# Layer 2's edge lookups in a two-layer graph attention kernel: another order of loads around them

## The chip, the cores and the metric

The kernel runs on one core of a Trainium2 chip. The metric is device time in microseconds. Three runs of the kernel before gave 1846.12, 1849.89 and 1850.75 us; their median, 1849.89 us, is the time before.

A core has five engines that run side by side: TensorE (PE in the profile) multiplies matrices, VectorE (DVE) does elementwise work and reductions, ScalarE (ACT) activations and copies, GpSimd (POOL) here mostly issues indirect DMAs (gathers), and SyncE (SP) issues plain DMAs. Each engine has its own instruction queue and keeps the order of that queue. The DMA transfers that SP, ACT and POOL issue share 16 DMA engines.

## The reference, cut to what matters

The input is a graph of 3125 nodes with 768 features each, and 53125 edges (25000 random ones, both ways, and a loop at each node), sorted by destination. A layer norm and a ReLU come first; then two graph attention layers (GAT). In short:

```
def gat_conv(x, edge_index, W, a_src, a_dst, bias, heads, out_ch, concat):
    src, dst = edge_index with a loop added at every node
    xl = (x @ W).reshape(n, heads, out_ch)
    alpha_src, alpha_dst = (xl * a_src).sum(-1), (xl * a_dst).sum(-1)
    e = leaky_relu(alpha_src[src] + alpha_dst[dst], 0.2)
    m = segment_max(e, dst)
    e = exp(e - m[dst])
    s = segment_sum(e, dst)
    alpha = e / (s[dst] + 1e-16)
    return segment_sum(xl[src] * alpha[:, :, None], dst) + bias

h0 = relu(layernorm(x))
h1 = relu(layer_norm(gat_conv(h0, ..., W1, heads=4, out_ch=256), g1, be1)) + (h0 @ Wr1 + br1)
h2 = layer_norm(gat_conv(h1, ..., W2, heads=1, out_ch=768), g2, be2) + (h1 @ Wr2 + br2)
out = x + h2
```

All matrices are float32. Layer 1 has 4 heads of 256 columns, layer 2 one head of 768. The edges' own order is kept in tiles: the nodes are split into 25 tiles of 128 destinations (the last one has 53), and a tile's edges fill up to 17 slots of 128 edges.

## The kernel before

Only layer 2 and the end of layer 1 are of interest. Layer 1 ends with its last tile's product with W2: the row of `xl` goes to the DRAM table `table2`, and the two numbers per node, alpha_src and alpha_dst, go to the SBUF tile `asad2` (L1261). Then layer 2 runs in three stages.

**Lookups** (`for b in range(NB)`, L1341 and on). For every edge slot of the 25 tiles, alpha_src of the source and alpha_dst of the destination are looked up with one-hot matrices, which layer 1 left in DRAM (`hot_d`, float8). For tile b, `load_hot` (L1283) brings one matrix `hot` of 405.1 KB into one of four buffers. `source_values` (L542) multiplies it with the table `tabs` on PE (51 small matmuls, L551), masks the result into `pick` on DVE (L553) and reduces it into `wide` (L556); `own_products` and `own_values` (L528, L539) do the same for the destinations (5 matmuls, then a reduction into the tile `own`). The first four matrices are loaded by POOL at the end of layer 1, behind eight pieces of the weights `wr2` (L1280, L1285); the other 21 by SP, each as soon as an earlier lookup has released its buffer.

**Shares** (`shares`, L643). The looked-up values become softmax weights: five transposes on PE (L673), two scans over the edges on DVE for the maximum per destination (L680, L681), six transposes back (L686), and some elementwise work, an exponential on ACT among it. `pen`, a mask, is loaded from DRAM by SP (L660).

**Sums** (`sums`, L703, called at L1376). For every tile and each of its slots POOL gathers 128 rows of `table2` (L774, tile `g`, 26 buffers, 416 gathers in this layer), DVE builds a weight matrix (L796), and PE adds the weighted rows into PSUM (L821). At a tile's end DVE adds the node's own row, which SP has loaded (`load_rows`, L191), normalizes, and ACT stores the tile of the output (`end2`, L1366).

**Residual.** `h1 @ Wr2` plus its biases is added to x. `load(b)` (L1291) loads a tile's h1 (512 KB) and x (384 KB) through SP, `residual` (L1300) does the matmuls in eight steps (L1307), a bias matmul (L1311) and two DVE adds into `xr` (L1316). It's a generator: each `next` does one step. `ahead_of(first, end, apart)` strings tiles together and loads two tiles ahead. Two tiles (`FIRST = 2`) are done ahead of the sums: a step after each lookup from b = 5 on, the rest in `shares`, whose last argument says how many steps stand behind the first transposes and how many behind the transposes back. The other 23 are spread evenly over the sums (`each`, L1359).

**What sets the order.** PE keeps the order in which the program is written; in the sums ACT and DVE do too. The other engines' queues are ordered by a planner, which runs a model of the machine at compile time and, whenever an engine is free, gives it the earliest written instruction that waits for nothing. A DMA that is written late but needs only a free buffer can so be issued early. `with tc.issue_after(ins):` puts the instructions written inside it behind `ins` where they are on the same engine. It's used once: the gathers (POOL) come after `behind`, a small copy on POOL that reads `wide` after the 18th lookup (b = 17, L1352).

Of the kernel before, what the change touches and what calls it, by code (L numbers as in the profile page):

```python
# [9 lines left out]
F32 = mybir.dt.float32  # L10
F32R = mybir.dt.float32r
BF16 = mybir.dt.bfloat16
# [17 lines left out]
J = 17  # L30
S = J * 128
# [4 lines left out]
WIN = 640  # L36
# [32 lines left out]
def in_order(  # L69
# [16 lines left out]
    nc = tc.nc  # L86
# [4 lines left out]
    C2 = W2.shape[1]  # L91
    P = 128
    NB = -(-N // P)
# [3 lines left out]
    NK1, NK2 = D // 128, HC // 128  # L97
# [18 lines left out]
    def rows_of(b):  # L116
        return P if b < NB - 1 else LAST

    def cols_of(i):
        return sum(rows_of(b) for b in late_in[i])  # L120
# [10 lines left out]
    h1T_d = dram.tile([NB, 128, NK2, P], F32, name="h1T_d")  # L131
# [9 lines left out]
    hot_d = dram.tile([NB, 128, HOT], F8, name="hot_d")  # L141
# [38 lines left out]
    def bcast(vec, n, parts=P):  # L180
        return bass.AP(tensor=vec.tensor, offset=vec.offset, ap=[[0, parts], [1, n]])
# [35 lines left out]
    def bias_rows(pool, name):  # L217
        t = pool.tile([2, C2], F32R, name=name)
        nc.sync.dma_start(t.bitcast(F32), parts_d)
        return t  # L220
# [616 lines left out]
    with tc.tile_pool(name="m1", bufs=1) as mp:  # L837
# [8 lines left out]
        with tc.tile_pool(name="h0", bufs=1) as hp, tc.tile_pool(name="pm1", bufs=1, space=PSUM) as pm1, \  # L846
# [5 lines left out]
            so = right.enter_context(tc.tile_pool(name="so1", bufs=1, side="right"))  # L852
            own = so.tile([128, J, 2 * H, NB], F32, name="own")
            tabs = so.tile([P, 3, H, NB], BF16, name="tabs")
            cnt = so.tile([128, NB], F32, name="cnt")
            with tc.tile_pool(name="w1", bufs=1) as wp, tc.tile_pool(name="d1", bufs=2) as dp, \
# [216 lines left out]
                fill = early()  # L1073
# [11 lines left out]
            with tc.tile_pool(name="pq1", bufs=1, space=PSUM) as pp:  # L1085
                with tc.tile_pool(name="sb1", bufs=1) as sb:
                    n = J * H * NB
                    pick = scr[:, :n].rearrange("p (j h b) -> p j h b", h=H, b=NB)
# [71 lines left out]
        with tc.tile_pool(name="w2", bufs=1, reuse_waits="tile") as wp, tc.tile_pool(name="e1", bufs=2, reuse_waits="tile") as ep, \  # L1160
# [3 lines left out]
            def load(i, k, q=nc.sync):  # L1164
                if i < NG:
                    n = cols_of(i)
                    t = loaded[i, k] = wp.tile([128, WIDE], F32, name="h0k", bufs=11)
                    q.dma_start(t[:, :n], h0T_d[i][:, k, :n])
# [98 lines left out]
    with tc.tile_pool(name="m2", bufs=1, reuse_waits="tile") as mp, \  # L1267
            tc.tile_pool(name="pr2", bufs=1, space=PSUM, reuse_waits="tile") as pr:
        al2 = mp.tile([128, J, 1, NB], F32, name="al2")
        ends2 = mp.tile([128, J, NB, 3], F32, name="ends2")  # L1270
        nc.vector.memset(ends2[:, :, :, 0:1], 1.0)
        ball_r = bias_rows(mp, "ball_r")
        b2_b = mp.tile([P, C2], F32, name="b2_b")
        g2_b = mp.tile([P, C2], F32, name="g2_b")
        wide = mp.tile([128, J, NB], F32, name="wide")
        FIRST = 2
        xrs = {0: mp.tile([128, C2], F32, name="xr", bufs=FIRST + 4)}
        wr2 = mp.tile([128, NK2, C2], F32, name="wr2")
        for k in range(NK2):
            nc.gpsimd.dma_start(wr2[:, k, :], Wr2[k * 128:(k + 1) * 128, :])  # L1280
        hots = {}

        def load_hot(b, q):  # L1283
            hots[b] = mp.tile([128, HOT], F8, name="hot", bufs=4)
            q.dma_start(hots[b][:, :S + WIN + J * NB], hot_d[b, :, :S + WIN + J * NB])  # L1285

        for b in range(4):
            load_hot(b, nc.gpsimd)
        loaded = {}

        def load(b):  # L1291
            if b < NB and b not in loaded:
                h1 = mp.tile([128, NK2, P], F32, name="h1", bufs=3)
                r = rows_of(b)
                nc.sync.dma_start(h1[:, :, :r], h1T_d[b][:, :, :r])
                xr = xrs[b] = xrs.get(b) or mp.tile([128, C2], F32, name="xr", bufs=FIRST + 4)
                load_rows(nc.sync, xr, x, b)
                loaded[b] = h1, xr

        def residual(b, apart):  # L1300

            h1, xr = loaded.pop(b)
            r = rows_of(b)
            pms = [pr.tile([P, 512], F32, name=f"pr{i}", bufs=2)[:r] for i in range(2)]
            for k in range(NK2):
                for i, pm in enumerate(pms):
                    nc.tensor.matmul(pm[:, :384], h1[:, k, :r], wr2[:, k, i * 384:(i + 1) * 384],  # L1307
                                     start=(k == 0), stop=False)
                yield
            for i, pm in enumerate(pms):  # L1310
                nc.tensor.matmul(pm[:, :384], ones_r[:, :r], ball_r[:, i * 384:(i + 1) * 384], start=False, stop=True)  # L1311
            for _ in range(apart):
                yield
            for i, pm in enumerate(pms):
                cs = slice(i * 384, (i + 1) * 384)
                nc.vector.tensor_add(xr[:r, cs], pm[:, :384], xr[:r, cs])  # L1316

        def ahead_of(first, end, apart):
            load(first)
            load(first + 1)  # L1320
            for b in range(first, end):
                load(b + 2)
                yield from residual(b, apart)

        with tc.tile_pool(name="ps2", bufs=1, space=PSUM, reuse_waits="tile") as pp:
            fill = ahead_of(0, FIRST, 5)
            with tc.tile_pool(name="so2", bufs=1, side="right", reuse_waits="tile") as so, \
                    tc.manual_schedule(engines={PE}):
                own = so.tile([128, J, 2, NB], F32, name="own")
                al = wide[:, :, None, :]  # L1330
                with tc.tile_pool(name="sb2", bufs=2, side="right", reuse_waits="tile") as sb:
                    part = parts_of(sb, asad2.rearrange("p b v -> p (b v)"), NB * 2, "part")
                    tabs = sb.tile([P, 3, 1, NB], BF16, name="tabs", bufs=1)
                    tabd = sb.tile([P, NB, 4, 3, 2], BF16, name="tabd", bufs=1)
                    v = lambda i: part[:, i, :].rearrange("p (b v) -> p b v", v=2)
                    by_quarter(tabd, v, NB, 1)
                    for i in range(3):
                        nc.vector.tensor_copy(tabs[:, i], v(i)[:, :, :1].rearrange("p b h -> p h b"))
                    for b in range(NB):
                        if b not in hots:  # L1340
                            load_hot(b, nc.sync)  # L1341
                        hot = hots.pop(b)
                        pick = sb.tile([128, J, 1, NB], F32, name="pick")
                        source_values(1, al, b, pp, 3, J, hot, tabs,
                                      hot[:, S + WIN:S + WIN + J * NB].rearrange("p (j b) -> p j b", b=NB), pick)
                        own_values(own, b, own_products(1, pp, hot[:, S:S + WIN], tabd[:, b]))
                        if b in (1, 2):
                            load(b - 1)
                        if b > 4:
                            next(fill)  # L1350
                        if b == NB - 8:
                            behind = nc.gpsimd.tensor_copy(mark, al[:, 0, 0, b:b + 1]).ins  # L1352
                with tc.tile_pool(name="sr2", bufs=1, side="right", reuse_waits="tile") as sr:
                    shares(wide, own, al2[:, :, 0, :], ends2, sr, pp, fill, (3, 2))
                for _ in fill:
                    pass

        more = ahead_of(FIRST, NB, 3)
        each = (NB - FIRST) * (NK2 + 3) / ((NB - 1.5) * len(ROUNDS))  # L1359

        with tc.tile_pool(name="w3", bufs=1, reuse_waits="tile") as wp, tc.tile_pool(name="e2", bufs=2, reuse_waits="tile") as ep, \
                tc.tile_pool(name="g2", bufs=1, reuse_waits="tile") as gp, tc.tile_pool(name="pg2", bufs=1, space=PSUM, reuse_waits="tile") as pp:
            nc.sync.dma_start(b2_b, bcast(b2, C2))
            nc.sync.dma_start(g2_b, bcast(g2, C2))

            def end2(b, z, share):  # L1366
                nc.vector.scalar_tensor_tensor(z, z, share, b2_b[:z.shape[0]], op0=OP.mult, op1=OP.add)  # L1367
                yield from norm_steps(ep, z, C2, 1)
                mu, rstd = norm_steps.found
                nc.vector.scalar_tensor_tensor(z, z, mu, g2_b[:z.shape[0]], op0=OP.subtract, op1=OP.mult)  # L1370
                nc.vector.scalar_tensor_tensor(z, z, rstd, xrs[b][:z.shape[0]], op0=OP.mult, op1=OP.add)
                yield
                store_rows(nc.scalar, out, b, z)

            with tc.issue_after(behind):
                sums(1, C2, table2, al2, ends2, 26, 1, gp, pp, end2, more, [each] * len(ROUNDS))  # L1376


# [470 lines left out]
```

## Time and profile before

| what | value |
|---|---|
| median of three runs | 1849.89 us |
| the profiled execution's own time | 1853.64 us |
| its span, first to last instruction | 1851.8 us |
| mean granted TensorE clock | 0.976 |
| PE busy | 1741.8 us (94% of the span) |
| DVE busy | 1063.1 us (57%) |
| POOL busy | 908.4 us (49%) |
| ACT busy | 296.2 us (16%) |
| DMA, mean over the span | 310 GB/s |
| first lookup, first gather, first sum of layer 2 | 1236.60, 1289.97, 1321.43 us |

Times in the profile are microseconds from the first instruction; "L1307" is a line of the kernel. An instruction group reads as line, engine, operation, output<-inputs, count; what stands in brackets or behind "<-" is what ended the idle time before it. "SPq" is SyncE's queue. The chain of waits follows the work that ended last back from the end. A row of a table by stage has the busy time (and number) of PE, PE's weight loads, DVE, ACT and POOL, then the granted clock (1.00 is full speed), the busy share of the DMA engines and what they moved. Matmuls are pipelined, so a busy PE isn't PE at its peak.

### The profile page before, as it was taken

To read this page: it belongs to the slowest core of one execution; us is meant where nothing else is said; L and a number is where in the kernel's file an instruction comes from. 1 tells how busy PE (TensorE), PEld (TensorE's weight loads), DVE (VectorE), ACT (ScalarE), POOL (GpSimd) and SP (SyncE) were. 2 spreads that over 40 slices of the span, in tenths; PEclk is the share of its full clock that TensorE was granted. 3 is DMA by queue.
4 is the path that set the end of the run, shared out by engine and by line. 5 is a ranking of instruction groups with operands and counts; after the bars stand their busy time and mean duration, and the time that the engine had idled before them with its cause. 6 is when DMAs were issued, how large, how long until landed. Compare 5 with 4: busy or idle time off the path is not lost. (4 is left out here: it accounts for less than half of the span.)

```text
span 1851.8 us, 34112 instructions
## 1 busy us (share of the span) xinstructions
PE 1741.8 (94%) x12558; PEld 965.8 (52%) x12558; DVE 1063.1 (57%) x3030; ACT 296.2 (16%) x1094; POOL 908.4 (49%) x981
## 2 busy tenths in 40 slices
PE   8999999999878999999999999979899999999996
PEld 5666665566434656556555555547444333334331
DVE  7683434888825465566566646534565444555555
ACT  2222331000211212112212112110111000001100
POOL 2000111111166666666666666501777777777774
PEclk9999999999989999999999999988899999999998
DMA  7824537776199999999999999937999999999996
GB/s 236 286 82 153 145 97 202 177 189 146 61 399 407 406 393 400 385 406 380 409 410 393 410 410 357 382 133 241 332 383 373 384 370 378 381 381 385 372 351 231
DMA packets 180209, 574.86 MB, mean 310 GB/s; under 512 B 32767, under 2 KB 54265, under 8 KB 179908
## 3 DMA queue, kind: packets, MB, share of 16 engines
q0 software_dynamic: 108432, 408.37, 59.5%
q1 hardware_dynamic: 68074, 154.62, 24.0%
q10 hardware_dynamic: 3530, 9.60, 1.3%
q8 instruction: 103, 1.69, 0.4%
q14 instruction: 70, 0.57, 0.1%
HBM read 503.27 MB, written 73.85 MB: 312 GB/s over the span
## 5 line engine op out<-in xcount | busy, mean ns | idle before, releaser
L774 POOL DMA_INDIRECT g<-table,idx_s x832 | 819.3, 985 | 416.4 <-issue 150.0
L821 PE MATMUL pa<-g,w 128*32 128x256 f32 (+2 forms) x5868 | 501.5, 426 | 50.8 <-DMA g<-table,idx_s 35.9
L821 PEld LDWEIGHTS pa<-g,w 128*32 128x32 f32 x5868 | 191.4, 110 | 328.7 <-issue 145.7
L1307 PE MATMUL pr<-wr,h 128*128 128x384 f32 (+1 forms) x800 | 290.7, 504 | 0.0
L1254 PE MATMUL p<-w,h1T 128*128 128x384 f32 (+2 forms) x800 | 280.4, 499 | 2.6 <-DVE h1T L1240 2.6
L796 DVE TENSOR_SCALAR w<-iota_f,rel_s,al 128x32 f32<-128x32 f32 (+1 forms) x416 | 104.1, 325 | 232.4 <-PE pa L821 231.9
L1307 PEld LDWEIGHTS pr<-wr,h 128*128 128x128 f32 (+1 forms) x800 | 141.8, 189 | 140.2 <-issue 59.7
L1254 PEld LDWEIGHTS p<-w,h1T 128*128 128x128 f32 (+1 forms) x800 | 144.9, 188 | 123.3 <-issue 26.4
L801 DVE TENSOR_TENSOR w<-oh,al 128x128 f32<-128x128 f32 (+1 forms) x416 | 132.0, 317 | 92.8 <-PE pa L821 59.9
L1185 PE MATMUL pr<-h0k,wr 128*128 128x256 f32 (+1 forms) x576 | 141.1, 393 | 0.0
L926 PE MATMUL pm<-w,h0l 128*128 128x344 f32 (+1 forms) x468 | 140.8, 455 | 0.0
L1063 PE MATMUL pm<-h0g,wr 128*128 128x512 f32 x288 | 133.1, 610 | 0.0
L926 PE MATMUL pm<-w,h0g 128*128 128x344 f32 x432 | 130.6, 458 | 0.3 <-ACT h0g L905 0.3
L1185 PEld LDWEIGHTS pr<-h0k,wr 128*128 128x128 f32 x576 | 106.9, 191 | 29.6 <-issue 9.8
L994 POOL DMA_DIRECT2D hot_d<-ohd x25 | 13.5, 540 | 220.1 <-DVE own L502 124.0
L800 DVE TENSOR_SCALAR oh<-iota_f,rel_s 128x32 f32<-128x32 f32 (+1 forms) x416 | 112.1, 269 | 0.1
L926 PEld LDWEIGHTS pm<-w,h0l 128*128 128x128 f32 (+1 forms) x468 | 84.8, 185 | 44.1 <-issue 5.7
L491 ACT ACTIVATE bn_sd<-bn_mv,eps 128x1 f32<-128x1 f32 (+1 forms) x50 | 14.7, 294 | 554.6 <-DVE bn_mv L487 537.8
L926 PEld LDWEIGHTS pm<-w,h0g 128*128 128x128 f32 x432 | 81.7, 193 | 40.6 <-issue 1.4
L1063 PEld LDWEIGHTS pm<-h0g,wr 128*128 128x128 f32 x288 | 53.6, 194 | 57.5 <-issue 57.2
L1238 ACT ACTIVATE h1T<-p,be_c,g_c 128x128 f32<-128x128 f32 (+1 forms) x200 | 72.2, 475 | 15.6 <-PE p L1233 12.5
L553 DVE TENSOR_TENSOR scr<-pq,ohh 128x500 f32<-128x500 f32 x100 | 56.8, 596 | 20.3 <-PE pq L551 20.3
(306 smaller groups left out, 1415.4 us busy)
## 6 DMA issues: line engine op xcount, KB each, us to landing
s<-slo_d SPq DMA_DIRECT2D x25, 544.0 KB
g<-table,idx_s POOLq DMA_INDIRECT x832
table<-row SPq DMA_DIRECT2D x24, 512.0 KB
own<-table SPq DMA_DIRECT2D x24, 512.0 KB
h1T_d<-h1T SPq DMA_DIRECT2D x24, 512.0 KB
h<-h1T_d SPq DMA_DIRECT2D x24, 512.0 KB
ring<-in_x_dram SPq DMA_DIRECT2D x24, 384.0 KB
table<-row SPq DMA_DIRECT2D x24, 384.0 KB
```

What stands on the lines that cost most here:

```text
L553: nc.vector.tensor_tensor(pick[:, j0:j0 + n], q, ohh[:, j0:j0 + n, None, :].to_broadcast([128, n, heads, NB]), OP.mult)
L774: nc.gpsimd.indirect_dma_start(out=g[:, :width], out_offset=None, in_=table[:, :], in_offset=bass.IndirectOffsetOnAxis(ap=idx_s[:, b * J + ...
L796: nc.vector.tensor_scalar(w[:, 0, :], iota_f[:, lo:hi], rel_s[:, c:c + 1], al[:, POS[j], 0, b:b + 1], op0=OP.is_equal, op1=OP.mult)
L800: nc.vector.tensor_scalar(oh, iota_f[:, lo:hi], rel_s[:, c:c + 1], None, op0=OP.is_equal)
L801: nc.vector.tensor_tensor(w, oh[:, None, :].to_broadcast([128, heads, hi - lo]), al[:, POS[j], :, b:b + 1].to_broadcast([128, heads, hi - ...
L821: nc.tensor.matmul(pa[32 * q:32 * q + 32, o // f, o % f:o % f + m], w[:, o // cols, :], g[:, o:o + m], start=to not in opened, stop=False, ...
L926: nc.tensor.matmul(pm[:r, :C], h0[b][:, k, :], w1[:, k, i * C:(i + 1) * C], start=(k == 0), stop=(k == NK1 - 1))
L1063: nc.tensor.matmul(pm, wr1[:, k, m * 128:(m + 1) * 128], groups[gi][:, k, :], start=(k == 0), stop=(k == NK1 - 1))
L1185: nc.tensor.matmul(pm[:, :n], wr1[:, k, m * 128:(m + 1) * 128], loaded[i, k][:, :n], start=(k == 0), stop=(k == NK1 - 1))
L1238: nc.scalar.activation(hT[:, k0 + k, :r], pt[:, k, :r], AF.Relu, bias=be1_c[:, k0 + k:k0 + k + 1], scale=g1_c[:, k0 + k:k0 + k + 1])
L1254: nc.tensor.matmul(pm[:, :n], hT[:, k, :r], w2[:, k, o:o + n], start=(k == 0), stop=(k == NK2 - 1))
L1307: nc.tensor.matmul(pm[:, :384], h1[:, k, :r], wr2[:, k, i * 384:(i + 1) * 384], start=(k == 0), stop=False)
```

## The change

Seven edits, all in layer 2:

- `own`, `pick`, `tabs` and `tabd` are allocated in the layer's main pool, not in pools on the other side of the memory that are closed after the lookups.
- POOL's loads at the end of layer 1 come in another order, the four matrices first and then the weights, and h1 of tiles 0 and 1 is added behind them (`load_h1`), no longer on SP.
- `FIRST` is 1: one tile's residual is done ahead of the sums, and 24 in them. There are five `xr` buffers, not six.
- `load(0)` is written after the 16th lookup (b = 15) and ordered behind the newest matrix's DMA (`last_hot`).
- Residual steps come only after the last three lookups (b = 22, 23, 24), with their loads behind `last_hot`; in `shares` five steps stand behind the first transposes and four behind the transposes back.
- The mark that lets the gathers begin is read after the 15th lookup (b = 14).
- The vectors b2 and g2, and all that `sums` issues on SP (own rows, h1 and x of later tiles), stand behind `last_hot`, by then the last matrix's DMA.

```diff
         wide = mp.tile([128, J, NB], F32, name="wide")
-        FIRST = 2
+        own = mp.tile([128, J, 2, NB], F32, name="own")
+        FIRST = 1
...
+        def load_hot(b, q):
+            hots[b] = mp.tile([128, HOT], F8, name="hot", bufs=4)
+            return q.dma_start(hots[b][:, :S + WIN + J * NB], hot_d[b, :, :S + WIN + J * NB]).ins
+
+        for b in range(4):
+            load_hot(b, nc.gpsimd)
+        picks = [mp.tile([128, J, 1, NB], F32, name="pick", bufs=2)]
+        tabs = mp.tile([P, 3, 1, NB], BF16, name="tabs")
+        tabd = mp.tile([P, NB, 4, 3, 2], BF16, name="tabd")
         for k in range(NK2):
             nc.gpsimd.dma_start(wr2[:, k, :], Wr2[k * 128:(k + 1) * 128, :])
...
+        def load_h1(b, q):
+            h1 = h1s[b] = mp.tile([128, NK2, P], F32, name="h1", bufs=3)
+            r = rows_of(b)
+            q.dma_start(h1[:, :, :r], h1T_d[b][:, :, :r])
+
+        for b in range(2):
+            load_h1(b, nc.gpsimd)
         loaded = {}
 
         def load(b):
             if b < NB and b not in loaded:
-                h1 = mp.tile([128, NK2, P], F32, name="h1", bufs=3)
-                r = rows_of(b)
-                nc.sync.dma_start(h1[:, :, :r], h1T_d[b][:, :, :r])
+                if b not in h1s:
+                    load_h1(b, nc.sync)
+                h1 = h1s.pop(b)
...
                         if b not in hots:
-                            load_hot(b, nc.sync)
+                            last_hot = load_hot(b, nc.sync)
...
-                        if b in (1, 2):
-                            load(b - 1)
-                        if b > 4:
-                            next(fill)
-                        if b == NB - 8:
+                        if b == NB - 10:
+                            with tc.issue_after(last_hot):
+                                load(0)
+                        if b > NB - 4:
+                            with tc.issue_after(last_hot):
+                                next(fill)
+                        if b == NB - 11:
                             behind = nc.gpsimd.tensor_copy(mark, al[:, 0, 0, b:b + 1]).ins
...
-                    shares(wide, own, al2[:, :, 0, :], ends2, sr, pp, fill, (3, 2))
+                    shares(wide, own, al2[:, :, 0, :], ends2, sr, pp, fill, (5, 4))
...
-            nc.sync.dma_start(b2_b, bcast(b2, C2))
-            nc.sync.dma_start(g2_b, bcast(g2, C2))
+            with tc.issue_after(last_hot):
+                nc.sync.dma_start(b2_b, bcast(b2, C2))
+                nc.sync.dma_start(g2_b, bcast(g2, C2))
...
-            with tc.issue_after(behind):
+            with tc.issue_after(behind), tc.issue_after(last_hot):
                 sums(1, C2, table2, al2, ends2, 26, 1, gp, pp, end2, more, [each] * len(ROUNDS))
```

More of the change, by code (lines that the diff above doesn't have):

```diff
@@ L1275, in in_order @@
         wide = mp.tile([128, J, NB], F32, name="wide")
-        FIRST = 2
+        own = mp.tile([128, J, 2, NB], F32, name="own")
+        FIRST = 1
         xrs = {0: mp.tile([128, C2], F32, name="xr", bufs=FIRST + 4)}
         wr2 = mp.tile([128, NK2, C2], F32, name="wr2")
-        for k in range(NK2):
-            nc.gpsimd.dma_start(wr2[:, k, :], Wr2[k * 128:(k + 1) * 128, :])
         hots = {}
@@ L1284, in load_hot @@
             hots[b] = mp.tile([128, HOT], F8, name="hot", bufs=4)
-            q.dma_start(hots[b][:, :S + WIN + J * NB], hot_d[b, :, :S + WIN + J * NB])
+            return q.dma_start(hots[b][:, :S + WIN + J * NB], hot_d[b, :, :S + WIN + J * NB]).ins
         for b in range(4):
             load_hot(b, nc.gpsimd)
+        picks = [mp.tile([128, J, 1, NB], F32, name="pick", bufs=2)]
+        tabs = mp.tile([P, 3, 1, NB], BF16, name="tabs")
+        tabd = mp.tile([P, NB, 4, 3, 2], BF16, name="tabd")
+        for k in range(NK2):
+            nc.gpsimd.dma_start(wr2[:, k, :], Wr2[k * 128:(k + 1) * 128, :])
+        h1s = {}
+        def load_h1(b, q):
[4 more added lines that the diff above has]
+            load_h1(b, nc.gpsimd)
         loaded = {}
@@ L1328, in in_order @@
                     tc.manual_schedule(engines={PE}):
-                own = so.tile([128, J, 2, NB], F32, name="own")
                 al = wide[:, :, None, :]
@@ L1332, in in_order @@
                     part = parts_of(sb, asad2.rearrange("p b v -> p (b v)"), NB * 2, "part")
-                    tabs = sb.tile([P, 3, 1, NB], BF16, name="tabs", bufs=1)
-                    tabd = sb.tile([P, NB, 4, 3, 2], BF16, name="tabd", bufs=1)
                     v = lambda i: part[:, i, :].rearrange("p (b v) -> p b v", v=2)
@@ L1340, in in_order @@
                         if b not in hots:
-                            load_hot(b, nc.sync)
+                            last_hot = load_hot(b, nc.sync)
                         hot = hots.pop(b)
-                        pick = sb.tile([128, J, 1, NB], F32, name="pick")
+                        pick = picks.pop() if picks else mp.tile([128, J, 1, NB], F32, name="pick", bufs=2)
                         source_values(1, al, b, pp, 3, J, hot, tabs,
```

## The prediction

> **What bounds the kernel now.** I read the page first, then a table by stage, the waits and timeline of GpSimd (POOL), the chain of waits around the change, and what SyncE's queue (SP) moved there. The page's span and three of its rows of 40 slices (46.3 us each):
>
> ```profile
> span 1851.8 us, 34112 instructions
> ...
> PE   8999999999878999999999999979899999999996
> ...
> POOL 2000111111166666666666666501777777777774
> ...
> GB/s 236 286 82 153 145 97 202 177 189 146 61 399 407 406 393 400 385 406 380 409 410 393 410 410 357 382 133 241 332 383 373 384 370 378 381 381 385 372 351 231
> ```
>
> Slices 27 to 29 (133, 241, 332 GB/s) are layer 2's lookups, the stage that is changed; POOL is idle in the first two. By stage, each row ends with the granted clock, DMA share and GB/s:
>
> ```profile
> 1200.00:1236.00 36.00, 31.66 (x110) 15.13 (x108) 9.27 (x27) 8.52 (x23) 0.00 (x0) 0.95 0.20 74
> ...
> 1236.50:1317.00 80.50, 64.00 (x1479) 51.30 (x1479) 41.32 (x93) 2.05 (x3) 21.12 (x22) 0.82 0.84 290
> ...
> 1480.00:1600.00 120.00, 115.63 (x615) 47.14 (x613) 60.56 (x185) 10.82 (x97) 91.96 (x93) 1.00 0.99 375
> ```
>
> In the sums POOL issues 93 gathers in 120 us, one per 1.29 us. Its longest wait late in the sums (1600 to 1800), then its timeline at both ends of the layer:
>
> ```profile
> POOL g L774 <- issue: 24.4, 80, 0.3
> ```
>
> ```profile
> 1288.97 0.18 POOL L1352 COPY mark<-wide 128x1 f32<-128x1 f32 x1 [92.38 <-DVE wide L556]
> 1289.97 1.02 POOL L774 DMA_INDIRECT g<-table,idx_s  x1 [0.82 <-DMA hot<-hot_d]
> ...
> 1324.46 0.94 POOL L774 DMA_INDIRECT g<-table,idx_s  x1 [1.04 <-PE pa L821]
> ...
> 1832.03 1.45 POOL L774 DMA_INDIRECT g<-table,idx_s  x1 [0.30 <-issue]
> ```
>
> A gather costs POOL 0.95 + 0.30 = 1.25 us; late in the sums it waits for nothing beyond that 0.30 us. The layer's gathers run from 1289.97 to 1833.48. There are 26 buffers, so POOL gets 26 x 1.25 = 32.5 us ahead and then stops until PE frees one, as at 1324.46. The first sum (1321.43, below) starts 31.5 us after the first gather. So two starts bind at once: the end moves by the smaller shift, that of the first gather or that of the first sum.
>
> The chain of waits through the stage:
>
> ```profile
> 1238.72 8.28 DMA xr<-in_x_dram
> ...
> 1247.08 8.16 DMA hot<-hot_d
> ...
> 1256.96 2.75 PE pr L1307 x4
> ...
> 1261.18 1.39 PE pr L1307 x4
> ...
> 1305.79 1.27 PE pq L551 x51
> ...
> 1307.19 1.39 PE pr L1307 x4
> 1308.58 0.61 PE pq L673 x5
> ...
> 1316.13 1.25 PE pq L686 x6
> 1317.38 4.06 issue
> 1321.43 4.00 PE pa L821 x16
> ```
>
> Two things lengthen it: one-hot matrices (hot) that queue behind rows of x and h1, and residual steps of 1.39 us between the lookups.
>
> **The change part by part.** *Loads out of the way.* PE idles 9.81 us for the fifth matrix; before it, lookups follow each other at VectorE's (DVE) pace:
>
> ```profile
> 1238.89 0.60 DVE L553 TENSOR_TENSOR pick<-pq,hot 128x425 f32<-128x425 f32 x1 [0.99 <-PE pq L551]
> ...
> 1240.38 0.60 DVE L553 TENSOR_TENSOR pick<-pq,hot 128x425 f32<-128x425 f32 x1 [0.22 <-PE pq L551]
> ...
> 1253.28 1.53 PE L551 MATMUL pq<-tabs,hot 128*128 128x25 bf16 x51 [9.81 <-DMA hot<-hot_d]
> ```
>
> With the rows held back, SP's next issue waits only for a pick to free one of four hot buffers. A matrix is 0.415 MB; undisturbed (1282 to 1290) SP's queue, q1, moved this in 8 us:
>
> ```profile
> q1 hardware_dynamic: 700, 2.07, 78.8%
> ...
> hot<-hot_d SPq DMA_DIRECT2D x5, 405.1 KB
> ```
>
> That is 259 GB/s, 1.6 us a matrix, against 1.49 us a lookup between the picks of 1238.89 and 1240.38. What is late next is the matrix itself. Without the 9.81 us and the residual steps, lookup 15's pick starts at 1238.89 + 3 x 1.49 + 11 x 1.6 = 1261; its two reductions add 1.3 us.
>
> *Gathers from the 15th lookup.* Mark to gather took 1.0 us, so the first gather goes from 1289.97 to about 1263.3: 26.7 us earlier. POOL then has its 26 buffers full by 1296 and stands still until the first sum.
>
> *What gathers do to the matrices.* This step decides. At the first gather 19 matrices are issued and six are to come. The residual's first loads are traced at the 23rd lookup and ordered behind the newest matrix of that point, the 23rd, not the 25th: x of tiles 1 and 2 and h1 of tile 2 then wait for nothing else, while matrices 24 and 25 wait for buffers. SP keeps order, so I count these three ahead of the last two. Their sizes:
>
> ```profile
> h<-h1T_d SPq DMA_DIRECT2D x24, 512.0 KB
> ...
> xr<-in_x_dram SPq DMA_DIRECT2D x24, 384.0 KB
> ```
>
> So SP must move 6 x 0.415 + 2 x 0.393 + 0.524 = 3.80 MB beside the gathers. The trace has such a stretch, 1292 to 1304, in which a matrix was always queued:
>
> ```profile
> DMA packets 1028, 4.17 MB, mean 347 GB/s; under 512 B 165, under 2 KB 204, under 8 KB 1026
> ...
> q0 software_dynamic: 602, 3.00, 70.7%
> q1 hardware_dynamic: 424, 1.13, 28.4%
> ```
>
> SP got 1.13 MB in 12 us, 94 GB/s; 3.80 MB take 40.4 us, to 1303.7. Counted the other way, 26 gathers of 0.393 MB and SP's share are 14.0 MB, at 347 GB/s also 40.4 us: no later is possible, since POOL stops at 26. From below, 259 GB/s gives 14.7 us, 1278. I take 1303.7, the row of the same two queues. The last lookup starts on PE near 1304.5, against 1305.79: **1.3 us** gained, 25 of the 26.7 spent waiting with full buffers.
>
> *One residual tile in the stage instead of two.* Three steps come with lookups 23 to 25; the last of these stands where 1307.19 stood. Five stand between the transposes of 1308.58 and 1316.13: 5 x 1.39 = 6.95 us, in a gap that DVE's scans made 6.94 us long (1309.19 to 1316.13). So 0 at full clock. But a step took 2.75 us at 1256.96, after lookups and waits alone, and 1.39 at 1261.18. If all six are at half clock, 6 x 1.36 = 8.2 us; none lost is the other end. By those two rows the clock is back about 4 us after steps begin, which costs one step, partly under DVE's scans: **0.7 us** lost. Two fewer adds on DVE gain nothing, PE being later.
>
> *The other tile* joins the sums: 8 x 1.39 and a bias matmul, 11.7 us of PE. From 1321 to 1835:
>
> ```profile
> L1307 PE MATMUL pr<-wr,h 128*128 128x384 f32 (+1 forms) x736 | 263.5, 500 | 0.0
> L821 PE MATMUL pa<-g,w 128*32 128x384 f32 (+1 forms) x1944 | 233.1, 496 | 23.4 <-DMA g<-table,idx_s 13.5 <-issue 4.1 <-DVE w L796 3.1
> ```
>
> PE waits 23.4 us there for gathers and weights. The tile fits in, at cost 0; if that cover were gone, 11.7.
>
> *Loads now after the last matrix:* two vectors, three own rows, two x tiles and an h1 tile, 7 x 0.393 + 0.524 = 3.28 MB, behind 1303.7 on SP. POOL is stopped then; at 375 GB/s they take 8.7 us and are there by 1313, before the first sum. Cost 0; up to 8.7 if gathers were still running. Their first readers are the ends of tile 0 and its residual.
>
> *Other edits together.* h1 of tiles 0 and 1 (1.05 MB) are two more DMAs on POOL's queue behind matrices and weights, in a stretch with a DMA share of 0.20: 0; if layer 1 still held their buffers they'd come with the first lookups, 1.05 MB at 259 GB/s, 4 us on matrix five. x of tile 0 follows the 16th matrix, 1.5 us on SP before gathers run, with no reader near. Own, picks and tables in another pool, and five x buffers instead of six, issue nothing: 0, and no gain either, as the first lookup waits for layer 1's last product.
>
> **Sum**, against the profiled run's 1853.64 us (span 1851.8): -1.3 + 0.7 = -0.6, 1853.0. The median of the runs is 1849.89, 3.75 us (0.2%) lower; from there 1849.3, and I predict 1849. A measurement here tells about 0.3%, 5.5 us, from no change.
>
> **The rivals.** *SP gets a bigger share beside gathers.* In the row, 424 packets of SP stood beside 602 of the gathers. With equal turns the mean packets, 2665 and 4983 bytes, would give SP 35% of 347 GB/s, 121: 3.80 MB in 31.4 us, the first sum 9 us earlier, 1840. Against it: 94 was measured with SP never empty. [...]
>
> *The three loads do come behind the last matrix.* Then 2.49 MB at 94 GB/s end at 1289.8, 14 us earlier: 1835. For it: only SP's order decides. Against it: before, too, x and own rows went out between matrices that waited for buffers:
>
> ```profile
> 1257.89 0.43 SPq L191 DMA_DIRECT2D xr<-in_x_dram  x1
> 1261.77 0.32 SPq L1285 DMA_DIRECT2D hot<-hot_d  x1
> 1262.14 0.43 SPq L191 DMA_DIRECT2D own<-table  x1
> ```
>
> *Gathers cost the matrices nothing.* All lookups run at 1.6 us, the first sum comes by 1293, and POOL never stops: 26.7 us, of which the DMA queues allow 21 (the stage's 290 GB/s x 80.5 us = 23.3 MB take 62.3 us at 375, and 1.05 MB left it): 1829. The 94 GB/s speak against it.
>
> *Slower: half clock through all six residual steps.* PE, which gets a matrix only every 4.4 us (0.415 MB at 94 GB/s), starts them cold, between the last matrix and the first sum, with nothing beside them. 8.2 instead of 0.7 us: 1857. It decides (5.5 us) from the fifth step at 2.75 us on. For it: 0.82 as the stage's clock; against it: 1261.18.
>
> **How the numbers follow.** First sum where it was: 0.41 (own range 1842 to 1857); bigger share 0.20; loads behind 0.10; no cost 0.07; half clock 0.22. Faster: 0.05 + 0.19 + 0.10 + 0.07 = 0.41. Same: 0.29 + 0.01 + 0.03 = 0.33. Slower: 0.07 + 0.19 = 0.26. The range leaves out the 1829 case and half of what lies above half clock: 1833 to 1859.
>
> **What would show it.** Right: a first gather near 1263, SP at about 94 GB/s until 1304, PE waiting several us per matrix for the last six, POOL idle over 20 us between its 26th and 27th gather, the first sum within 3 us of 1321. Wrong: lookups over by 1290, or six residual steps at 2.75 us. The whole falls if the first sum moves by over 6 us, or if the end doesn't follow it.

## The result, and the profile after

The changed kernel takes **1840.70 us** (median of nine runs, 1839.92 to 1842.61) against 1850.75 us of the kernel before beside it (nine runs, 1846.12 to 1858.27): ratio 0.9943, with a 95% interval of 0.9930 to 0.9955. It is faster by 0.6%. The profiled execution of it took 1842.33 us.

The page of the changed kernel: its span, and PE, POOL and the DMA rate in 40 slices of 46.0 us.

```profile
span 1840.5 us, 34112 instructions
...
PE   7999999999878999999999999987799999999996
...
POOL 2000111111076566666666666603477777777774
...
GB/s 236 284 87 151 140 108 194 187 186 152 43 391 407 407 390 401 385 405 387 404 411 399 410 410 361 383 123 299 318 383 388 379 390 384 389 380 383 370 355 231
```

POOL's slices 27 to 29 now read 0, 3 and 4, where they read 0, 1 and 7: the gathers begin earlier, and then POOL stops. The span is 11.3 us shorter. POOL's timeline shows the two ends of the layer's gathers, and the first gather that had to wait for a sum, the 27th:

```profile
1265.63 0.18 POOL L1364 COPY mark<-wide 128x1 f32<-128x1 f32 x1 [39.81 <-DVE wide L556]
1266.61 1.02 POOL L774 DMA_INDIRECT g<-table,idx_s  x1 [0.79 <-DMA hot<-hot_d]
...
1315.83 0.94 POOL L774 DMA_INDIRECT g<-table,idx_s  x1 [14.01 <-PE pa L821]
...
1821.30 0.95 POOL L774 DMA_INDIRECT g<-table,idx_s  x1 [0.30 <-issue]
```

The first gather moved by 23.4 us (1289.97 to 1266.61), the 27th by 8.6 us (1324.46 to 1315.83). POOL gave 14.01 us of its lead back standing still with 26 full buffers. From the 27th gather to the last, POOL took 505.5 us, where it had taken 507.6.

The chain of waits through the stage: start, length, and what it was.

```profile
1267.05 6.39 DMA hot<-hot_d
...
1275.73 17.99 DMA hot<-hot_d
...
1293.77 1.54 PE pq L551 x51
1295.44 2.47 PE pr L1320 x4
1297.91 1.27 PE pq L551 x51
1299.30 1.39 PE pr L1320 x4
...
1301.30 6.45 PE pr L1320 x20
...
1308.83 3.98 issue
1312.81 4.00 PE pa L821 x16
```

The first sum starts at 1312.81, 8.6 us earlier than before, and that is the shift of the 27th gather. Two matrices carry most of the chain: the one issued at 1275.73 is on its way for 17.99 us. What stands ahead of it in SyncE's queue is in SP's timeline:

```profile
1260.67 12.34 SPq L1284 DMA_DIRECT2D hot<-hot_d  x7
1273.06 0.46 SPq L191 DMA_DIRECT2D xr<-in_x_dram  x1
1273.57 0.44 SPq L1298 DMA_DIRECT2D h<-h1T_d  x1
1274.05 0.49 SPq L191 DMA_DIRECT2D xr<-in_x_dram  x1
1275.73 3.88 SPq L1284 DMA_DIRECT2D hot<-hot_d  x2
```

These are x, h1 and x of the residual, and behind them matrices 24 and 25. What the queues moved from 1276 to 1292 (packets, MB, share of the 16 engines' time; q0 is the gathers, q1 is SP):

```profile
DMA packets 1642, 6.49 MB, mean 406 GB/s; under 512 B 257, under 2 KB 257, under 8 KB 1640
...
q0 software_dynamic: 821, 4.04, 62.9%
q1 hardware_dynamic: 819, 2.42, 38.5%
```

SP got 2.42 MB in 16 us, **151 GB/s**, and the two queues sent nearly the same number of packets, 819 and 821.

### The profile page after: what moved, and what is told of

Same layout as the page of the kernel before. It is cut to its first block, busy times and chain, and to the rows that moved or that the text cites. A ratio compares the mean times of both kernels' runs of the same rounds, so it can differ in the third digit from the quotient of the medians.

```text
span 1840.5 us, 34112 instructions
## 1 busy us (share of the span) xinstructions
PE 1729.5 (94%) x12558; PEld 965.4 (52%) x12558; DVE 1060.9 (58%) x3030; ACT 296.2 (16%) x1094; POOL 905.0 (49%) x983
## 5 line engine op out<-in xcount | busy, mean ns | idle before, releaser
L821 PE MATMUL pa<-g,w 128*32 128x256 f32 (+2 forms) x5868 | 486.4, 426 | 50.7 <-DMA g<-table,idx_s 39.7
```

The costliest lines, as they stand in the source:

```text
L821: nc.tensor.matmul(pa[32 * q:32 * q + 32, o // f, o % f:o % f + m], w[:, o // cols, :], g[:, o:o + m], start=to not in opened, stop=False, ...
```

## The experiments

Theory A: the end is set by the 27th gather, which comes at the later of two times, that of the first sum and that of 26 gathers after the first one. In the changed kernel the first sum is the later, and it waits for the last matrices in SP's queue. Theory B: what counts is how early the gathers begin.

The profiled executions don't begin layer 2 at the same time (the first lookup starts at 1237.05 us in the changed kernel and at 1241.27 in e5, in which nothing is changed ahead of it), so the table counts from each kernel's first lookup on PE:

| kernel | first lookup, us of the span | first gather | first sum | 27th gather | end of the span | median, us | ratio to before, 95% |
|---|---|---|---|---|---|---|---|
| before | 1236.60 | 53.4 | 84.8 | 87.9 | 615.2 | 1850.75 | |
| changed | 1237.05 | 29.6 | 75.8 | 78.8 | 603.5 | 1840.70 | 0.9943 (0.9930 to 0.9955) |
| e1_behind_last | 1239.91 | 30.6 | 67.7 | 70.8 | 593.4 | 1833.24 | 0.9897 (0.9869 to 0.9924) |
| e2_gathers_18 | 1241.23 | 34.8 | 72.4 | 75.4 | 596.4 | 1839.53 | 0.9928 (0.9900 to 0.9957) |
| e3_both | 1237.34 | 35.8 | 66.8 | 73.3 | 598.2 | 1837.68 | 0.9925 (0.9897 to 0.9953) |
| e4_early_alone | 1237.91 | 48.4 | 84.8 | 87.8 | 614.6 | 1854.04 | 1.0010 (0.9993 to 1.0027) |
| e5_extra_tile | 1241.27 | 30.1 | 76.3 | 79.3 | 605.9 | 1844.54 | 0.9951 (0.9933 to 0.9969) |
| e6_split | 1237.80 | 30.6 | 83.9 | 87.0 | 610.4 | 1850.76 | 0.9991 (0.9972 to 1.0009) |
| e7_two_parts | 1239.35 | 24.8 | 70.8 | 73.8 | 598.6 | 1836.86 | 0.9908 (0.9880 to 0.9935) |
| e8_x0_too_16 | 1240.39 | 31.8 | 67.2 | 70.3 | 594.3 | 1836.20 | 0.9910 (0.9887 to 0.9933) |

Runs e1 to e4 shared one chip, on which the kernel before took 1851.40 us (median of 13), e5 to e8 another, 1853.32 us (median of 19). Across the groups the ratios are compared.

**e1_behind_last: the residual's three loads behind the last matrix.** x of tiles 1 and 2 and h1 of tile 2 are held and issued after the 25th matrix. Nothing else changes.

```diff
+        held = []
...
-                if b not in h1s:
+                if b == 2:
+                    h1s[b] = mp.tile([128, NK2, P], F32, name="h1", bufs=3)
+                    held.append((nc.sync.dma_start, h1s[b], h1T_d[b]))
+                elif b not in h1s:
                     load_h1(b, nc.sync)
...
-                load_rows(nc.sync, xr, x, b)
+                if b in (1, 2):
+                    held.append((load_rows, nc.sync, xr, x, b))
+                else:
+                    load_rows(nc.sync, xr, x, b)
...
+                        if b == NB - 1:
+                            with tc.issue_after(last_hot):
+                                for f, *a in held:
+                                    f(*a)
```

> The changed kernel with x of tiles 1 and 2 and h1 of tile 2 held back behind the 25th matrix instead of the 23rd. Theory A (the end follows the later of two starts, the first sum and the 27th gather's earliest time, and matrices 24 and 25 are what the first sum waits for): 1.31 MB less in front of them, at the 151 GB/s that SP got beside gathers in the changed kernel 8.7 us, so the first sum goes from 1312.8 to about 1304, and the time from 1840.7 to about 1832. Theory B (the gain came from gathers that start earlier): the first gather stays near 1266.6, and so the time at 1841.

Measured 1833.24 us, near theory A's 1832 and far from B's 1841. Counted from the first lookup, the first gather is 1.1 us later than in the changed kernel, the first sum and the 27th gather are 8.0 us earlier, and the end follows these. SP's and POOL's timelines of e1:

```profile
1265.05 17.82 SPq L1284 DMA_DIRECT2D hot<-hot_d  x9
1282.92 0.45 SPq L191 DMA_DIRECT2D xr<-in_x_dram  x1
```

```profile
1310.68 0.94 POOL L774 DMA_INDIRECT g<-table,idx_s  x1 [4.55 <-PE pa L821]
```

The last nine matrices go out in one run, and POOL's stop has shrunk from 14.01 to 4.55 us. This is the fastest version of the study by its ratio, 1.0% under the kernel before, though the intervals of e7 and e8 overlap its own.

**e2_gathers_18: the changed kernel, but gathers from the 18th lookup, as before.**

```diff
-                        if b == NB - 11:
+                        if b == NB - 8:
```

> The changed kernel with the gathers let go after the 18th lookup, as before, instead of the 15th. Theory A: the first gather comes 5 us later, near 1272, the matrices have the queues to themselves for as long (259 instead of 151 GB/s), so the first sum comes 3 to 4 us earlier, near 1309; POOL still has its 26 buffers full by then; time about 1837. Theory B: 5 us later, 1846.

Measured 1839.53 us, 2.5 us over A's 1837. The first gather was 5.2 us later than in the changed kernel, and by theory B the time would be 1846. B is refuted: the earlier mark of the change bought nothing. By its trace it cost something, as A has it: without it the first sum and the 27th gather came 3.4 us earlier. In the ratios that is 2.8 us (0.9928 for 0.9943), which the intervals don't separate from none.

**e3_both: both edits together.**

> Both edits: the three loads behind the 25th matrix, gathers from the 18th lookup. Theory A: lookups end near 1285, the first sum could come near 1300, and now the gathers bind: 1272 + 26 x 1.25 = 1304.5; 27th gather near 1305.5 instead of 1315.8; time 1830 to 1832, no better than the first edit alone. Theory B: 1846.

Measured 1837.68 us, 6 us over the expectation. The first sum did move, by 8.9 us from the changed kernel, but the 27th gather only by 5.5. Its rows on PE and POOL:

```profile
1304.18 4.01 PE L821 MATMUL pa<-g,w 128*32 128x384 f32 x16 [4.00 <-issue]
```

```profile
1308.78 0.95 POOL L774 DMA_INDIRECT g<-table,idx_s  x1 [0.31 <-issue]
1310.65 0.94 POOL L774 DMA_INDIRECT g<-table,idx_s  x1 [0.92 <-DMA g<-table,idx_s]
```

Here the gathers are the later: the 26th ends at 1309.73, after the first sum began, and the 27th waits 0.92 us for an earlier gather's DMA, no longer for a sum. The 26 gathers from 1273.17 to the 27th took 37.5 us, not the 32.5 us at 1.25 us each that I had counted: seven waits end with an earlier gather's DMA (0.30 to 0.92 us each, 4.1 in all), and one gather took POOL 2.69 us. So in e3 the second of the two times binds, and its 27th gather is 2.5 us later than e1's; its median is 4.4 us higher. The rest may lie behind the 27th gather, where e3 took 524.9 us to the end and e1 522.6; over the ten kernels this stretch took 521.0 to 527.3 us, and what makes these differences was not looked into.

**e4_early_alone: the kernel before, with gathers from the 15th lookup.**

> The kernel before with one edit, gathers from the 15th lookup instead of the 18th. Theory A: the first gather moves 8 us forward (three lookups at 2.78 us), to 1281.6, but the matrices then come one per 2.75 us beside gathers, just the pace of the lookups with their residual steps; first sum 1321 to 1325, time 1850 to 1854, no gain. Theory B: 8 us faster, 1842.

Measured 1854.04 us, ratio 1.0010: no gain, as A expects. The first gather came 5.0 us earlier (8.4 were expected), the first sum and the 27th gather not at all:

```profile
1325.72 0.94 POOL L774 DMA_INDIRECT g<-table,idx_s  x1 [5.87 <-PE pa L821]
```

The lead went into POOL's stop (1.04 us before, 5.87 here).

**e5_extra_tile: is a residual tile in the sums free?** The eight residual steps of tile 12 are done twice, inside the sums; the first result is written over. The spacing of the steps (`each`) allows for the eight more.

```diff
+                if b == 12:
+                    h1 = loaded[b][0]
+                    for _ in residual_again(h1):
+                        yield
...
-        each = (NB - FIRST) * (NK2 + 3) / ((NB - 1.5) * len(ROUNDS))
+        each = ((NB - FIRST) * (NK2 + 3) + NK2) / ((NB - 1.5) * len(ROUNDS))
```

> The changed kernel with the residual matmuls of one more tile (tile 12, its eight steps) done a second time inside the sums, into a scratch result that the first pass writes over; the output is unchanged. Eight steps are about 11 us of TensorE at its full clock (the sums' residual steps at 1.39 us each). Theory A (the end is set by POOL's gathers once the sums have begun; TensorE has idle time in every tile, 24.6 us waiting for gathers and 18.3 us of other idle in the sums): the extra tile costs nothing, 1841 us (1838 to 1844). Rival (TensorE and POOL are so near to each other that a tile more in the sums is paid in full or half): 1846 to 1852 us.

Measured: ratio 0.9951 (0.9933 to 0.9969) beside the changed kernel's 0.9943, a difference of 1.5 us in a stretch that got 11.4 us of PE work more. (Its median, 1844.54, is just over the 1838 to 1844 expected; the kernel before took 1853.32 beside it.) From the 27th gather to the end its profiled execution took 526.7 us, 2.0 us more than the changed kernel's, within the spread given above. The sums' groups on PE, first in the changed kernel and then in e5:

```profile
L821 PE MATMUL pa<-g,w 128*32 128x387 f32 (+1 forms) x1956 | 221.5, 496 | 24.6 <-DMA g<-table,idx_s 18.3 <-issue 4.0 <-DVE w L796 1.6
```

```profile
L821 PE MATMUL pa<-g,w 128*32 128x384 f32 (+1 forms) x1956 | 218.2, 496 | 19.4 <-DMA g<-table,idx_s 12.6 <-issue 4.0 <-DVE w L796 1.6
...
L1335 PE MATMUL pr<-wr,h 128*128 128x384 f32 x32 | 11.4, 499 | 0.0
```

PE's waits for gathers fell from 18.3 us in the changed kernel to 12.6. So half of the tile's 11.4 us took the place of waits for gathers; where the rest went wasn't looked into. The rival's full price of 11 us is excluded. Half of it, some 5.7 us, lies at the edge of what the two intervals allow.

**e6_split: shorter packets for SP.** Matrices 20 to 25 are loaded as two transfers of half the columns.

```diff
-            return q.dma_start(hots[b][:, :S + WIN + J * NB], hot_d[b, :, :S + WIN + J * NB]).ins
+            n = S + WIN + J * NB
+            cuts = (0, n) if b < 19 else (0, n // 2, n)
+            for o, e in zip(cuts, cuts[1:]):
+                ins = q.dma_start(hots[b][:, o:e], hot_d[b, :, o:e]).ins
+            return ins
```

> The changed kernel with the 20th to 25th one-hot matrix each loaded as two transfers of half the columns, so that SP's packets are half as long and twice as many. In the changed kernel SP and POOL moved 819 and 821 packets in 1276 to 1292 us, 2.42 and 4.04 MB. Theory of equal turns by packet: SP's share beside the gathers falls from 151 to some 80 to 105 GB/s, the last 2.49 MB take 7 to 12 us longer, the first sum moves from 1312.8 to about 1320, and the time goes to about 1848 us (1846 to 1851). Rival (the share goes by bytes or by requests, packet length is of no account): first sum at 1313, 1841 us.

Measured 1850.76 us, ratio 0.9991: with the same bytes in the same order the whole gain of the change is gone. The queues from 1284 to 1300, and PE's waits for matrices from 1236 to 1313:

```profile
q0 software_dynamic: 895, 4.41, 69.2%
q1 hardware_dynamic: 904, 1.96, 32.4%
```

```profile
PE pq L551 <- DMA hot<-hot_d: 18.2, 10, 6.4
```

The packets are nearly equal in number again, 904 to 895, but SP's are shorter (2170 bytes in the mean for 2950), so SP moved 122 GB/s instead of 151. The total hardly changed (400 GB/s, 406 in the changed kernel), so it's SP's share that fell. Ahead of this stretch, from 1276 to 1284, SP sent 615 packets and the gathers 456, so the numbers weren't equal from the first gather on. PE waited 18.2 us for matrices, for 9.3 in the changed kernel, and the first sum came 8.2 us later after the first lookup. The 122 GB/s are over the 80 to 105 that I expected, but this stretch holds many whole rows among SP's packets. From 1294 to 1302 most of them are halves:

```profile
DMA packets 969, 3.17 MB, mean 396 GB/s; under 512 B 151, under 2 KB 525, under 8 KB 969
...
q0 software_dynamic: 487, 2.40, 75.9%
q1 hardware_dynamic: 482, 0.77, 27.0%
```

There SP got 0.77 MB in 8 us, 96 GB/s, as expected. The rival, that packet length is of no account, is refuted.

**e7_two_parts: fewer PE instructions in a lookup.** The source lookup leaves out the third, smallest bf16 part of the table.

```diff
-                for i in range(3):
+                parts = 2 if heads == 1 else 3
+                for i in range(parts):
...
-                                     tabs[:, i], start=(i == 0), stop=(i == 2))
+                                     tabs[:, i], start=(i == 0), stop=(i == parts - 1))
```

> The changed kernel with layer 2's source lookup made from two of the three bf16 parts of its table: the third, smallest part is left out, and with it 17 of the 51 matmuls and as many weight loads of that product in each lookup (78 PE instructions a lookup for 112). Theory that TensorE's stalls in the lookups (8.4 us put down to issue, in nine places 256 PE instructions apart) go with the number of instructions and set the pace: the stalls fall to 2 to 6 us, the first gather comes 2 to 4 us earlier (1262.5 to 1264.5 for 1266.6), the first sum at 1308 to 1311, and the time is 1836 to 1839 us. Rival (the one-hot matrices' stream sets the pace and the stalls lie in time that TensorE would have waited anyway): first gather within 1 us of 1266.6, first sum at 1312 to 1313.5, 1840 to 1842 us.

Measured 1836.86 us, ratio 0.9908, some 6.5 us under the changed kernel by the ratios. PE's waits in the lookups:

```profile
PE pq L552 <- DMA hot<-hot_d: 21.1, 12, 7.6
...
PE pq L552 <- issue: 1.2, 1, 1.2
```

Counted from the first lookup, the first gather came 4.7 us earlier than in the changed kernel, the first sum and the 27th gather 5.0 us. So PE, and not the matrices' stream, set the pace of the lookups ahead of the gathers. Whether by the stalls or by the work isn't told apart: 17 matmuls fewer a lookup are also 15 x 17 x 28 ns = 7 us less matmul time ahead of the mark (51 in 1.43 us), and PE's waits for matrices rose by 11.8 us.

**e8_x0_too_16: e1 with x of tile 0 behind the last matrix too, and gathers from the 16th lookup.**

> The kernel of e1_behind_last with x of tile 0 held behind the 25th matrix as well, and gathers from the 16th lookup for the 15th. In e1 the 27th gather waited 4.55 us for the first sums, so gathers had that much slack; the one later lookup takes some 1.6 us of it, and beside fewer gathers the last matrices come faster. Theory A (the later of first sum and gathers decides, and here it is still the first sum): first sum 0 to 2 us earlier than in e1 (1307.6), 1831 to 1833 us. Rival (gathers decide already, each lookup of delay is paid): 1834.5 to 1836 us.

Measured 1836.20 us, ratio 0.9910 beside e1's 0.9897: nothing gained, and no difference from e1 that the intervals show. The first sum and the 27th gather come 0.5 us earlier than in e1, as theory A has it, and POOL still waits 3.58 us for the sums ahead of its 27th gather, so the rival's mechanism isn't there. The time itself fits the rival's 1834.5 to 1836 and misses A's 1831 to 1833; by the ratio, on e1's chip, it would be 1834.7.

## Why the prediction was right in its range and wrong in its likeliest case

The time fell inside the range and on the faster side, but the likeliest case (1849, first sum unmoved) didn't happen. What did is the first rival, "SP gets a bigger share beside gathers", and at its time, 1840. Step by step:

*Two starts bind, and the end moves by the smaller shift:* right. First gather 23.4 us earlier, first sum 8.6, 27th gather 8.6. Over the ten kernels the 27th gather comes 70.3 to 87.9 us after the first lookup, and the end 521.0 to 527.3 us after that gather. The last 2.7 us of the 11.3 lie behind the 27th gather and within that spread, so they aren't put down to the change.

*The first gather near 1263:* 1266.61, 3.3 us late. The lookups were to run at 1.6 us, the matrices' pace. What I missed are PE's own stops, which the section on the hardware shows: five of them, 4.2 us in all, lie ahead of the 15th lookup. With fewer instructions, e7 is 4.7 us quicker to the first gather, though it can't tell the stops from the work that it saves.

*SP's order (two x and an h1 ahead of matrices 24 and 25):* right to the row. The rival that they come behind, for which I gave 1835, is e1: 1833.24.

*SP at 94 GB/s beside gathers until 1303.7:* **this is the term that failed.** It measured 151 GB/s from 1276 to 1292. The premise "a matrix was always queued" in the stretch 1292 to 1304 of the kernel before was false. What the queues moved there from 1293 to 1296, and what SP's queue waited for from 1286 to 1300:

```profile
q0 software_dynamic: 182, 0.90, 94.6%
q1 hardware_dynamic: 18, 0.05, 7.5%
```

```profile
SPq L1285 <- DVE pick L553: 9.5, 5, 3.3
```

For three of the twelve microseconds SP sent almost nothing: its next load had stood waiting for a pick to free a buffer. Nor was much left to send. SP's timeline from 1293 to 1304 has the last two matrices and the small `pen`, and nothing else:

```profile
1293.84 3.11 SPq L1285 DMA_DIRECT2D hot<-hot_d  x2
1297.00 2.05 SPq L660 DMA_DIRECT2D pen<-near_d  x4
```

PE set the pace of these loads, as each lookup had a residual step behind it. PE's timeline of the kernel before:

```profile
1294.49 1.43 PE L551 MATMUL pq<-tabs,hot 128*128 128x25 bf16 x51
1295.77 0.27 PE L534 MATMUL pd<-tabd,hot 128*128 128x24 bf16 x5
1295.90 1.54 PE L1307 MATMUL pr<-wr,h 128*128 128x384 f32 x4
1297.27 1.44 PE L551 MATMUL pq<-tabs,hot 128*128 128x25 bf16 x51
```

That is 2.78 us a lookup (1294.49 to 1297.27), with no wait at all for a matrix. SP's 1.13 MB were these two matrices (0.83 MB), the rest of the ones before them and `pen`, all that it had been given to load. So 94 GB/s doesn't show what the DMA engines would have given SP; a rate is a price only where the queue has work all the time. Nor do the row's 424 packets to 602 speak against equal turns: without the three microseconds they are 406 to 420, and the 281 to 375 from 1297 to 1304 fall where SP had at most these two matrices and `pen` on the way. In the changed kernel no residual step stands behind lookups 1 to 22, other loads follow the matrices in SP's queue, and from 1276 to 1292 the two queues sent nearly equal numbers of packets, 819 to 821. That is what the rival's equal turns would give, and e6 has 904 to 895 with packets of other lengths (1284 to 1300). That the queues take turns stays the rival's assumption: how they are served, no run here shows, and over other stretches the numbers aren't equal, 1410 to 1171 in the changed kernel from 1266.6 to 1293.7 (below) and 615 to 456 in e6 from 1276 to 1284.

Even so the rival's terms were off. What SP and the gathers moved in the changed kernel from its first gather to the start of the 24th lookup, 1266.6 to 1293.7:

```profile
q0 software_dynamic: 1171, 5.81, 53.6%
q1 hardware_dynamic: 1410, 4.13, 42.8%
```

The rival had 3.80 MB at 121 GB/s, 31.4 us from 1263.3; SP moved 4.13 MB at 152 GB/s, 27.1 us from 1266.6. 121 came from the total of the same bad stretch, 347 GB/s, where the full queues moved 406. That both end near 1294 is partly luck.

*No later than 40.4 us, since POOL stops at 26 gathers:* the bound held, as did "POOL stops"; the stop was 14.01 us and not over 20, since the first sum came earlier than I thought.

*Residual steps, 0.7 us lost:* right in size. The step after the 24th lookup took 2.47 us, 1.1 us more than the next, which was back at 1.39; the granted clock was 0.56 from 1295.3 to 1297.8 and 1.00 from there to 1300.6. From the last lookup's start to the first sum it took 14.90 us (1297.91 to 1312.81), for 15.64 before, so 0.7 came back. The rival of half clock through all six steps is refuted: five steps of 6.45 us stand in the chain.

*One tile more in the sums, 0:* right, by e5 within what it can tell (1.5 us, and not 11).

*h1 by POOL, x of tile 0, loads after the last matrix, other pools, 0:* nothing in the chain or in the waits shows a cost. The sums' first start waits only for the 3.98 us of issue that stood there before (4.06). These weren't tried one by one. Nor does any run separate what the matrices without rows ahead of them and the lookups without residual steps each gave to the 8.6 us.

## What to carry to other kernels

A transfer rate taken from a trace is a price only if the queue had work throughout (94 GB/s here where SP sent almost nothing for three of twelve microseconds, 151 where its loads stood in line): look for packets in each microsecond and for what the issuing engine waits for before using it. When a producer that runs ahead into a fixed number of buffers is made to start earlier, its lead is lost in the stop at the full buffers unless the consumer's first start moves too (here 14.01 of 23.4 us were lost); in e1 three loads, each about as large as a matrix, moved behind the last matrix were worth some 8 us, and in e2 letting the gathers go 5 us later cost nothing. In the changed kernel from 1276 to 1292 and in e6 from 1284 to 1300 the two queues sent nearly equal numbers of packets (819 to 821, 904 to 895), and the gathers, whose packets were the longer, moved 4.04 MB to SP's 2.42 and 4.41 to 1.96.

## What the runs showed of the hardware that I had not expected

With the lookups packed close, PE stopped in the middle of a lookup for something that the trace puts down to "issue" alone. PE's waits in the lookups, 1236 to 1313, of the kernel before and of the changed one (total us, times, longest):

```profile
PE pq L551 <- issue: 0.6, 1, 0.6
```

```profile
PE pq L551 <- issue: 8.4, 9, 1.9
```

Two neighbouring stops in PE's timeline of the changed kernel:

```profile
1244.41 0.79 PE L551 MATMUL pq<-tabs,hot 128*128 128x25 bf16 x25 [0.58 <-issue]
...
1246.60 1.27 PE L551 MATMUL pq<-tabs,hot 128*128 128x25 bf16 x42
1248.97 0.42 PE L551 MATMUL pq<-tabs,hot 128*128 128x25 bf16 x9 [1.09 <-issue]
```

A lookup has 112 instructions on PE (51 source and 5 own matmuls, each with a weight load). From the first stop to the second come 2 x 25 + 2 x 5, a whole lookup of 112, and 2 x 42: 256. The seven other distances between the nine stops, counted the same way, are 256 too. What stops PE there, no run here shows. In e7 the 25 lookups have 78 x 25 = 1950 instructions, room for seven such distances, and only one stop of 1.2 us is left; so not every 256th instruction brings a stop.
